# The last expert pair's two tiles in a bank each, and an instruction order drawn with 0.7 instead of 0.8 before TensorE

## The chip, the core and the metric

The kernel runs on one core of a Trainium2 chip. TensorE (PE in the profile) multiplies matrices and writes its results to PSUM, which the kernel divides into eight banks of 128 partitions by 512 floats. VectorE (DVE) and ScalarE (ACT) take results out of the banks. GpSimd (POOL) issues the indirect transfers (gather and scatter), SyncE (SP) the plain ones. The metric is the time of one execution on the device in microseconds (us).

## What is computed

One layer on 2 x 2048 tokens of width 256. The normalised tokens `xn` go through a causal attention made of Chebyshev polynomials and prefix sums, and, in parallel, through a mixture of eight experts, of which each token takes one, plus a shared expert that every token takes:

```python
xn  = _layernorm(x, axis=-1)
x   = x + attn(xn, W_in, W_out) + ffn(xn, ...)
# in ffn, with xf = layernorm(xn) * ln_w + ln_b:
top_idx   = argmax(xf @ router_w, axis=-1);  top_score = sigmoid(max(xf @ router_w))
for e in range(8):
    w    = where(top_idx == e, top_score, 0)[:, None];  xe = xf * w
    acc += (silu(xe @ gate_w[e]) * (xe @ up_w[e])) @ down_w[e]
shared = silu(xf @ sh_gate) * (xf @ sh_up) @ sh_down
```

All of it is in 32-bit floats.

## The kernel before

The tokens are worked in eight chunks `c` of 512 (`NC`), each of four tiles of 128. For every chunk there is a front (normalise, transpose, router), an attention part (`attend`: projections at L1019, head sums at L1049, L1062 and L1067, denominators at L1130 and L1143, output at L1157) and a shared expert (`shared`: gate and up at L955, down at L973). A routing step sorts the tokens into slots by expert. The routed work is then done in units: nine pairs (`pair`: two full tiles of one expert side by side; gate and up at L1258, down at L1271), and single tiles (`expert`: transposes at L1297 and L1320, gate and up at L1307, down at L1328), some of whose tiles are cut into strips of 32 or 64 tokens of different experts. The small matmuls, on 32 or 64 columns of the array, are the head sums and such strips.

A unit ends with a copy of its result from PSUM to a buffer `yt` (L1274 for a pair, L1331 for a single tile) and a scatter to `y_dram` at the tokens' places (`scatter`, L1212, on POOL). The scatters carry a common key, "scatter", so that each waits until the one before it has landed. When all of them have landed, SP loads `y_dram` back in eight pieces (L1354), DVE adds each piece to its chunk `X` (L1363) and SP stores the chunk (L1367). The last chunk is stored in three pieces, and its last two tiles have separate down products and separate adds (L979 to L982), which end the program.

No engine's order is written out by hand. Every step is an `op` with an engine, a cost, the keys it reads and writes, the buffers it takes, and a priority. `Plan.order` plays the steps through in the program's own time: whenever an engine is free, it takes the ready step with the lowest priority number. A step is ready when its inputs are done, plus 0.2 between engines (`CROSS`), or plus 0.8 (`SLACK`) where the step is TensorE's; a buffer or bank is given out again 0.2 after its last user, and the first free one in its pool is taken. The constants decide the order and the places alone; on the chip each engine runs its list in order and waits for semaphores. A change of one constant can therefore move any step on any engine, and give any step another bank.

`bank_p` holds six of the eight PSUM banks; `psq` and `psk` are the other two. In the last pair as in all others, both tiles' down products go to the two halves of one bank `py`, one copy takes the whole bank (ACT, or DVE if it is free first), and two scatters follow.

Of the kernel before, what the change touches and what calls it, by code (L numbers as in the profile page):

```python
# [20 lines left out]
P = 128  # L21
NB, S, D = 2, 2048, 256
# [16 lines left out]
NPAIR = (4 * NTT - 7 * NE) // 8  # L39
# [63 lines left out]
class Plan:  # L103
# [2 lines left out]


    CROSS = 0.2
    SLACK = 0.8
    LAND = 2.2  # L110
    RATE = 280e3
    TABLE = 1.3
# [4 lines left out]
    def op(self, eng, cost, emit, r=(), w=(), a=(), prio=0.0, alloc=(), nbytes=None, alt=(), table=None,  # L117
           after=(), grow=None):

        o = Op()
        o.seq, o.prio, o.alloc, o.nbytes, o.table, o.grow = len(self.ops), prio, list(alloc), nbytes, table, grow
        o.alts = [(eng, cost, emit)] + list(alt)
        need = {}
        for k in r:
            need.update(dict.fromkeys(self.adds.get(k, ())))
            if k in self.last:
                need[self.last[k]] = None
            self.reads.setdefault(k, []).append(o)  # L130
        for k in a:
            if k in self.last:
                need[self.last[k]] = None
            need.update(dict.fromkeys(self.reads.get(k, ())))
            self.adds.setdefault(k, []).append(o)
        for k in w:
            if k in self.last:
                need[self.last[k]] = None
            need.update(dict.fromkeys(self.reads.get(k, ())))
            need.update(dict.fromkeys(self.adds.get(k, ())))  # L140
            self.last[k], self.reads[k], self.adds[k] = o, [], []
        need.pop(o, None)
        o.soon = [n for n in after if n not in need]
        need.update(dict.fromkeys(after))
        o.need, o.after, o.done = need, [], None
        o.bufs = {}
        for k in tuple(r) + tuple(w) + tuple(a):
            b = k[0] if isinstance(k, tuple) else k
            if isinstance(b, Buf):
                o.bufs[b] = None  # L150
        for b in o.alloc:
            b.owner = o
        for b in o.bufs:
            b.users += 1
            if b.owner is not o:
                need[b.owner] = None
        self.ops.append(o)
        return o

    def order(self):  # L160
# [13 lines left out]
        def lat(a, b):  # L174
            return 0.0 if a == b else self.SLACK if b == "PE" else self.CROSS

# [82 lines left out]
def kernel(  # L259
# [107 lines left out]
    bank_p = Pool([ps.tile([P, CH], F32, name=f"bank_{i}") for i in range(6)])  # L367
# [6 lines left out]
    op = plan.op  # L374
    V, A, G, S_, T_ = nc.vector, nc.scalar, nc.gpsimd, nc.sync, nc.tensor
    MM, M256, MT = 0.86, 0.442, 0.115
    KiB = 1024


    FRONT, ROUTE, SCAT, EXQ, SHQ, ATT, EXP, SHA = 0.0, 2.0, 4.0, 6.0, -1.0, 10.0, 30.0, 50.0  # L380
# [10 lines left out]
    for c in range(NC):  # L391
        if c == 0:
            for t in range(NT):
                op("SP", 0.45, lambda t=t: S_.dma_start(out=X[0][:, t, :], in_=x[ts(t, P)]),
                   w=[("X", 0, t)], nbytes=128 * KiB, prio=-90)
# [5 lines left out]
               table="sqrt")  # L401
# [3 lines left out]
               w=["sg"], nbytes=512 * KiB, prio=-88)  # L405
            op("SP", 0.45, lambda: S_.dma_start(out=su, in_=sh_up.rearrange("(k p) f -> p k f", p=P)),
               w=["su"], nbytes=512 * KiB, prio=-87)
        else:
            op("SP", 0.45, lambda c=c: S_.dma_start(
                out=X[c], in_=x[c * CH : (c + 1) * CH].rearrange("(t p) d -> p t d", p=P)),  # L410
               w=[("X", c, t) for t in range(NT)] + [("x_in", c)], nbytes=512 * KiB, prio=-80 + 5 * c)
        if c == 1:
            op("SP", 0.45, lambda: S_.dma_start(out=sd, in_=sh_down.rearrange("(k p) d -> p k d", p=P)),
               w=["sd"], nbytes=512 * KiB, prio=-73)
            op("SP", 0.45, lambda: S_.dma_start(out=w_in, in_=w_in_t.rearrange("(k p) e -> p k e", p=P)),
               w=["w_in"], nbytes=768 * KiB, prio=-74)
        if c == 2:
            op("SP", 0.45, lambda: S_.dma_start(out=w_out, in_=w_out_t.rearrange("(k p) e -> p k e", p=P)),
               w=["w_out"], nbytes=256 * KiB, prio=-68)
# [783 lines left out]
    def gather(e, j, zt):  # L1203
        op("POOL", 1.28, lambda: G.indirect_dma_start(  # L1204
            out=zt.t, out_offset=None, in_=z_dram,
            in_offset=bass.IndirectOffsetOnAxis(ap=take_i[:, j : j + 1], axis=0),
            bounds_check=NTOK - 1, oob_is_err=False,
        ), r=["table"] + [("z_dram", c) for c in range(NC)], w=[zt], alloc=[zt], nbytes=1024 * KiB, prio=EXQ + e - 0.05)

    def scatter(j, yt, src):  # L1210
        def f():
            y_ins.append(G.indirect_dma_start(  # L1212
                out=y_dram, out_offset=bass.IndirectOffsetOnAxis(ap=give_i[:, j : j + 1], axis=0),
                in_=src(), in_offset=None, bounds_check=NTOK - 1, oob_is_err=False,
            ).ins)

        op("POOL", 1.28, f, r=[yt, "table"], w=[("y", j), "scatter"], nbytes=640 * KiB, prio=SCAT)

    def pair(n, j):


        e = 0.1 * n
        ws = [Buf(w_p, f"{m}_{j}") for m in ("wg", "wu", "wd")]
        wg, wu, wd = ws
        zts = [Buf(zt_p, f"zt_{j + i}") for i in range(2)]
        sc = Buf(zt_p, f"sc_{j}")
        xT, yt = Buf(h_p, f"xT_{j}"), Buf(h_p, f"yt_{j}")
        pz, py = Buf(bank_p, f"pz_{j}"), Buf(bank_p, f"py_{j}")
        weights(e, [j // 2], [ws])
        for i in range(2):  # L1230
            gather(e, j + i, zts[i])
        op("POOL", 1.0, lambda: G.dma_start(
            out=sc.t.rearrange("p (i q) -> p i q", i=2),
            in_=score_dram[j : j + 2].unsqueeze(0).to_broadcast([P, 2, P])),
           r=["score_dram"], w=[sc], alloc=[sc], nbytes=128 * KiB, prio=EXQ + e - 0.04)
        for i in range(2):
            def f(i=i):
                for k in range(KD):
                    T_.transpose(pz.t[:, ds(k * 2 * P + i * P, P)], zts[i].t[:, ts(k, P)], ident)  # L1239
            op("PE", 2 * MT, f, r=[zts[i]], w=[(pz, i)], alloc=[] if i else [pz, xT], prio=EXQ + e)  # L1240
        for k in range(KD):
            op("ACT", 0.46, lambda k=k: A.activation(
                xT.t[:, ts(k, 2 * P)], pz.t[:, ts(k, 2 * P)], AF.Identity, bias=lnb[:, k : k + 1],
                scale=lnw[:, k : k + 1]), r=[(pz, 0), (pz, 1), "ln"], w=[(xT, k)], prio=EXQ)

        def f():
            v = xT.t.rearrange("p (k t) -> p k t", k=KD)
            V.tensor_tensor(v, v, sc.t.unsqueeze(1).to_broadcast([P, KD, 2 * P]), ALU.mult)
        X2 = [(xT, 0), (xT, 1)]
        op("DVE", 0.69, f, r=X2 + [sc], w=X2, prio=EXQ)  # L1250
        sls = []
        for h in range(2):
            pg, pu, sl = Buf(bank_p, f"eg_{j + h}"), Buf(bank_p, f"eu_{j + h}"), Buf(h_p, f"sl_{j + h}")

            def mm(b, wt, h=h):
                for f in range(2):
                    for k in range(KD):
                        T_.matmul(b.t[:, ts(f, 2 * P)], wt.t[:, ds(k * FF + (2 * h + f) * P, P)], xT.t[:, ts(k, 2 * P)],  # L1258
                                  start=(k == 0), stop=(k == KD - 1))
            op("PE", 4 * M256, lambda mm=mm, pg=pg: mm(pg, wg), r=X2 + [wg], w=[pg], alloc=[pg, pu], prio=EXP + e)  # L1260
            o = op("PE", 4 * M256, lambda mm=mm, pu=pu: mm(pu, wu), r=X2 + [wu, pg], w=[pu], prio=EXP + e - 0.2)
            op("ACT", 0.62, lambda sl=sl, pg=pg: A.activation(sl.t, pg.t, AF.Silu), r=[pg], w=[sl], alloc=[sl],
               prio=EXQ, table="silu")
            op("DVE", 0.69, lambda sl=sl, pu=pu: V.tensor_tensor(sl.t, sl.t, pu.t, ALU.mult), r=[pu, sl], w=[sl],
               prio=EXQ)
            sls.append(sl)
        ups.append(o)
        for i in range(2):
            def f(i=i):
                for f in range(KF):  # L1270
                    T_.matmul(py.t[:, ts(i, D)], sls[f // 2].t[:, ds(f % 2 * 2 * P + i * P, P)], wd.t[:, ts(f, D)],  # L1271
                              start=(f == 0), stop=(f == KF - 1))
            op("PE", 4 * M256, f, r=sls + [wd], w=[(py, i)], alloc=[] if i else [py], prio=EXQ + 10 + e)
        op("ACT", 0.6, lambda: A.copy(yt.t, py.t), r=[(py, 0), (py, 1)], w=[yt], alloc=[yt], prio=EXQ,  # L1274
           alt=[("DVE", 0.69, lambda: V.tensor_copy(yt.t, py.t))])
        for i in range(2):
            scatter(j + i, yt, lambda i=i: yt.t[:, ts(i, D)])

    def expert(n, j):
        e = 0.1 * n  # L1280
# [44 lines left out]
        def f():  # L1325
# [6 lines left out]
           alt=[("DVE", 0.42, lambda: V.tensor_copy(yt.t, py.t[:, :D]))])  # L1332

        scatter(j, yt, lambda: yt.t)


# [13 lines left out]
    for c in range(NC):  # L1350
        b = Buf(w_p, f"y_{c}")

        def f(c=c, b=b):
# [11 lines left out]
           r=[b], a=keys, prio=60 + c)  # L1365
        for t, n in ((0, 2), (2, 1), (3, 1)) if c == NC - 1 else ((0, NT),):
            op("SP", 0.45, lambda c=c, t=t, n=n: S_.dma_start(  # L1367
                out=out[ds(c * CH + t * P, n * P)].rearrange("(t p) d -> p t d", p=P), in_=X[c][:, t : t + n, :]),
               r=keys[t : t + n], w=[("out", c, t)], nbytes=n * 104 * KiB, prio=60 + c)
# [40 lines left out]
```

## Time and profile before

| | us |
|---|---|
| median of 3 runs | 564.18 (564.17 to 564.25) |
| the profiled execution | 564.25 |
| its span, first to last instruction | 562.5 |
| PE busy | 554.8 |
| DVE busy | 489.0 |
| ACT busy | 222.1 |
| POOL busy | 101.0 |

The span leaves out 1.75 us of the execution that lie before its first and after its last instruction. The granted TensorE clock is 0.998 of full speed over the span. TensorE's busy time counts from the start of a weight load or matmul to its modelled end, so that pieces which stand close together merge into one; a matmul of 32-bit floats shows as two instructions, and a group marked x8 is four matmuls.

### The profile page before, as it was taken

To read this page: it belongs to the slowest core of one execution; us is meant where nothing else is said; L and a number is where in the kernel's file an instruction comes from. 1 tells how busy PE (TensorE), PEld (TensorE's weight loads), DVE (VectorE), ACT (ScalarE), POOL (GpSimd) and SP (SyncE) were. 2 spreads that over 40 slices of the span, in tenths; PEclk is the share of its full clock that TensorE was granted. 3 is DMA by queue.
4 is the path that set the end of the run, shared out by engine and by line. 5 is a ranking of instruction groups with operands and counts; after the bars stand their busy time and mean duration, and the time that the engine had idled before them with its cause. 6 is when DMAs were issued, how large, how long until landed. Compare 5 with 4: busy or idle time off the path is not lost.

```text
span 562.5 us, 8132 instructions
## 1 busy us (share of the span) xinstructions
PE 554.8 (99%) x2760; PEld 324.5 (58%) x2760; DVE 489.0 (87%) x814; ACT 222.1 (39%) x430; POOL 101.0 (18%) x123
## 2 busy tenths in 40 slices
PE   7999999999999999999999999999999999999996
PEld 7564465665457575556547545756645474368754
DVE  6899898998999999999999989899999989677236
ACT  4869761012552344235333524442363353212000
POOL 4210100005142330231114122113101100112100
PEclk9999999999999999999999999999999999999999
DMA  8857651147658993884499287829836871950098
GB/s 277 284 169 261 226 225 37 45 147 266 184 193 286 313 367 89 275 276 170 145 352 327 87 272 262 304 57 316 293 102 209 275 261 24 297 194 19 27 296 302
DMA packets 78505, 119.71 MB, mean 213 GB/s; under 512 B 5416, under 2 KB 47199, under 8 KB 78464
## 3 DMA queue, kind: packets, MB, share of 16 engines
q1 hardware_dynamic: 73504, 107.49, 56.7%
q0 software_dynamic: 4416, 11.70, 6.9%
q8 instruction: 22, 0.36, 0.3%
q14 instruction: 19, 0.16, 0.1%
q10 hardware_dynamic: 544, 0.00, 0.1%
HBM read 100.28 MB, written 19.16 MB: 212 GB/s over the span
## 4 chain that ended last, share of the span: by engine, by line
PE 98%; DVE 1%; DMA 0%; ACT 0%; issue 0%
PE bank L955 20%; PE bank L1019 15%; PE bank L1258 11%; PE bank L1307 11%; PE bank L973 10%; PE bank L1271 6%; PE bank L1328 6%; PE bank L1157 5%; PE psk L1049 3%; PE psq L1049 2%; PE bank L1320 1%; PE bank L557 1%; PE psk L1062 1%; PE bank L1239 1%; PE bank L897 1%; PE psk L1143 1%
## 5 line engine op out<-in xcount | busy, mean ns | idle before, releaser
L1019 PE MATMUL bank<-xnT,w_in 128*128 128x512 f32 x192 | 87.3, 595 | 0.0
L1086 DVE TENSOR_TENSOR_SCAN tv<-ones,carry,tv 128x512 f32<-128x512 f32 x60 | 76.7, 1278 | 1.0
L1307 PE MATMUL bank<-big,wide 128*32 128x512 f32 (+2 forms) x288 | 64.0, 598 | 0.0
L1212 POOL DMA_INDIRECT y_dram<-wide,give_i x28 | 33.7, 1205 | 166.2 <-ACT wide L1274 63.2
L955 PE MATMUL bank<-xfT,sg 128*128 128x512 f32 (+1 forms) x136 | 60.8, 572 | 1.1 <-ACT xfT L535 1.1
L955 PE MATMUL bank<-xfT,su 128*128 128x512 f32 (+1 forms) x136 | 61.0, 573 | 0.0
L1258 PE MATMUL bank<-wide,big 128*128 128x256 f32 x256 | 58.5, 381 | 0.0
L1019 PEld LDWEIGHTS bank<-xnT,w_in 128*128 128x128 f32 x192 | 35.5, 190 | 39.8 <-issue 36.2
L973 PE MATMUL bank<-sd,hT 128*128 128x256 f32 x256 | 57.8, 381 | 0.0
L1258 PEld LDWEIGHTS bank<-wide,big 128*128 128x128 f32 x256 | 47.9, 190 | 10.5 <-issue 3.9
L973 PEld LDWEIGHTS bank<-sd,hT 128*128 128x128 f32 x256 | 47.8, 190 | 8.8 <-issue 1.6
L962 ACT ACTIVATE hT<-bank 128x512 f32<-128x512 f32 x32 | 19.0, 596 | 75.5 <-PE bank L955 75.4
L1106 DVE TENSOR_TENSOR o<-o,tv 128x512 f32<-128x512 f32 x64 | 44.2, 691 | 1.5
L1204 POOL DMA_INDIRECT wide<-z_dram,take_i x20 | 25.2, 1258 | 89.0 <-DVE give_i L922 72.9
L955 PEld LDWEIGHTS bank<-xfT,sg 128*128 128x128 f32 x136 | 24.6, 190 | 26.6 <-issue 23.5
L955 PEld LDWEIGHTS bank<-xfT,su 128*128 128x128 f32 x136 | 24.8, 190 | 24.2 <-issue 22.4
L1041 DVE SCALAR_TENSOR_TENSOR T<-T 128x1024 f32<-128x1024 f32 x32 | 37.8, 1216 | 0.0
L1027 ACT ACTIVATE T<-bank 128x512 f32<-128x512 f32 x32 | 19.1, 596 | 45.3 <-PE bank L1019 45.1
L1307 PEld LDWEIGHTS bank<-big,wide 128*32 128x32 f32 (+2 forms) x288 | 19.1, 128 | 29.0 <-issue 27.6
L964 DVE TENSOR_TENSOR hT<-hT,bank 128x512 f32<-128x512 f32 x32 | 21.8, 683 | 12.4 <-PE bank L955 12.4
L1083 DVE TENSOR_TENSOR tv<-T 128x512 f32<-128x512 f32 x48 | 32.4, 674 | 0.1
L990 DVE TENSOR_TENSOR X<-X,bank 128x512 f32<-128x512 f32 x31 | 21.1, 680 | 11.9 <-PE bank L973 7.8
(266 smaller groups left out, 923.1 us busy)
## 6 DMA issues: line engine op xcount, KB each, us to landing
big<-in_up_w SPq DMA_DIRECT2D x47, 512.0 KB, 5.4
big<-in_gate_w SPq DMA_DIRECT2D x41, 512.0 KB, 5.7
big<-in_down_w SPq DMA_DIRECT2D x40, 512.0 KB, 6.4
z_dram<-big SPq DMA_DIRECT2D x8, 512.0 KB, 4.5
xfT<-in_down_w SPq DMA_DIRECT2D x8, 512.0 KB, 5.4
X<-in_x SPq DMA_DIRECT2D x7, 512.0 KB, 9.3
xn_dram<-xnT SPq DMA_DIRECT2D x7, 512.0 KB, 3.3
xnT<-xn_dram SPq DMA_DIRECT2D x7, 512.0 KB, 8.6
```

The source lines that it names most:

```text
L955: T_.matmul(b.t[:, cols], wt[:, k, ts(f, P)], vx(k)[:, cols], start=(k == 0), stop=(k == KD - 1))
L973: T_.matmul(po.t[:, ts(i, D)], hT[f].t[:, ts(tp * 2 + i, P)], sd[:, f, :], start=(f == 0), stop=(f == KF - 1))
L1019: T_.matmul(pm.t, w_in[:, k, ds(i * D + g * P, P)], xnT.t[:, ts(k, CH)], start=(k == 0), stop=(k == KD - 1))
L1041: op("DVE", 1.27, lambda i=i, j=j, q=part: V.scalar_tensor_tensor(q[i](), q[j](), off[i], q[1](), ALU.subtract, ALU.mult), r=[(T, j)] + X2 ...
L1083: V.tensor_tensor(b.t, q[i](1), v(), ALU.mult)
L1086: o_ = op("DVE", 1.25, lambda b=b, i=i, g=g: V.tensor_tensor_scan(b.t, ones[:, 0:1].to_broadcast([P, CH]), b.t, 0.0 if opening else old[:, ...
L1106: op("DVE", 0.66, lambda o=o, b=b: V.tensor_tensor(o(), o(), b.t, ALU.add), r=[b, ok], w=[ok], prio=p)
L1212: y_ins.append(G.indirect_dma_start(out=y_dram, out_offset=bass.IndirectOffsetOnAxis(ap=give_i[:, j : j + 1], axis=0), in_=src(), in_offse ...
L1258: T_.matmul(b.t[:, ts(f, 2 * P)], wt.t[:, ds(k * FF + (2 * h + f) * P, P)], xT.t[:, ts(k, 2 * P)], start=(k == 0), stop=(k == KD - 1))
L1271: T_.matmul(py.t[:, ts(i, D)], sls[f // 2].t[:, ds(f % 2 * 2 * P + i * P, P)], wd.t[:, ts(f, D)], start=(f == 0), stop=(f == KF - 1))
L1307: T_.matmul(b.t[n, :], xT.t[:, ds(k * P + n.start, n.stop - n.start)], wt.t[:, ts(k, FF)], start=(k == 0), stop=(k == KD - 1), skip_group_ ...
L1328: T_.matmul(py.t[n, :D], hmT.t[:, ds(i * P + n.start, n.stop - n.start)], wd.t[:, ts(i, D)], start=(i == 0), stop=(i == KF - 1), skip_grou ...
```

## The change

`SLACK` is 0.7 instead of 0.8, so every step of every engine is ordered anew. In the last pair (`j == 2 * NPAIR - 2`), the two tiles take a bank each (`pys`), ACT copies each tile's 128x256 result by itself after that tile's four down matmuls, and each scatter waits for its own copy; DVE is no longer an alternative for these copies. The other pairs are written as before.

```diff
-    SLACK = 0.8
+    SLACK = 0.7
...
-    def scatter(j, yt, src):
+    def scatter(j, yt, src, key=None):
...
-        op("POOL", 1.28, f, r=[yt, "table"], w=[("y", j), "scatter"], nbytes=640 * KiB, prio=SCAT)
+        op("POOL", 1.28, f, r=[key or yt, "table"], w=[("y", j), "scatter"], nbytes=640 * KiB, prio=SCAT)
...
+        last = j == 2 * NPAIR - 2
+        pys = [py, Buf(bank_p, f"py_{j + 1}")] if last else [py, py]
         for i in range(2):
             def f(i=i):
                 for f in range(KF):
-                    T_.matmul(py.t[:, ts(i, D)], sls[f // 2].t[:, ds(f % 2 * 2 * P + i * P, P)], wd.t[:, ts(f, D)],
+                    T_.matmul(pys[i].t[:, ts(i, D)], sls[f // 2].t[:, ds(f % 2 * 2 * P + i * P, P)], wd.t[:, ts(f, D)],
                               start=(f == 0), stop=(f == KF - 1))
-            op("PE", 4 * M256, f, r=sls + [wd], w=[(py, i)], alloc=[] if i else [py], prio=EXQ + 10 + e)
-        op("ACT", 0.6, lambda: A.copy(yt.t, py.t), r=[(py, 0), (py, 1)], w=[yt], alloc=[yt], prio=EXQ,
-           alt=[("DVE", 0.69, lambda: V.tensor_copy(yt.t, py.t))])
+            op("PE", 4 * M256, f, r=sls + [wd], w=[(pys[i], i)], alloc=[] if i and not last else [pys[i]],
+               prio=EXQ + 10 + e)
+            if last:
+                op("ACT", 0.4, lambda i=i: A.copy(yt.t[:, ts(i, D)], pys[i].t[:, ts(i, D)]), r=[(pys[i], i)],
+                   w=[(yt, i)], alloc=[] if i else [yt], prio=EXQ)
+        if not last:
+            op("ACT", 0.6, lambda: A.copy(yt.t, py.t), r=[(py, 0), (py, 1)], w=[(yt, 0), (yt, 1)], alloc=[yt], prio=EXQ,
+               alt=[("DVE", 0.69, lambda: V.tensor_copy(yt.t, py.t))])
         for i in range(2):
-            scatter(j + i, yt, lambda i=i: yt.t[:, ts(i, D)])
+            scatter(j + i, yt, lambda i=i: yt.t[:, ts(i, D)], (yt, i))
```

The lines behind the pair move down by up to eight: L1271 becomes L1274, the whole-bank copy L1282, the single copies L1279, L1297 becomes L1305, L1307 L1315, L1320 L1328, L1322 L1330, L1328 L1336, L1354 L1362, L1363 L1371 and L1367 L1375. The text below uses the numbers of before, except where it says otherwise.

## The prediction
> **What bounds the kernel now.** I read the page's busy times first, then the chain that ended last, then the chain in order of time, then the timeline and the windows of the last 35 us.
>
> ```profile
> PE 554.8 (99%) x2760; PEld 324.5 (58%) x2760; DVE 489.0 (87%) x814; ACT 222.1 (39%) x430; POOL 101.0 (18%) x123
> ...
> PE 98%; DVE 1%; DMA 0%; ACT 0%; issue 0%
> ```
>
> TensorE is the bound, and hardly ever waits: 98% of the chain is its own work. So there is almost no wait to win, and whatever lengthens TensorE's list lengthens the kernel. The chain in order of time shows what on that list isn't multiplication:
>
> ```profile
> 213.76 1.00 PE psk L1049 x8
> 214.76 0.86 PE psq L1049 x8
> 215.62 3.65 PE bank L1258 x16
> ...
> 429.71 0.59 ACT wide L1322
> 430.35 1.99 PE bank L1328 x8
> ...
> 511.17 3.45 PE bank L1258 x16
> ```
>
> Columns: start, length, piece. L1258 x16 takes 3.45 us among full matmuls (the last line), but 3.65 with a group of 32-column matmuls before and after it; L1049 x8 takes 1.00 as the first such group, 0.86 as the second. One visit to the small matmuls thus costs 0.20 + 0.14 = 0.34 us beyond its work, however long it is. ACT in the chain is the one real wait after the first 9 us: L1328 waits for the copy L1322. By the starts, the L1130 group ahead of it occupies 0.84 us where its six other visits alone take 0.45, so the wait is 0.39.
>
> The end, by the timeline:
>
> ```profile
> 528.91 0.69 DVE L1275 COPY tv<-bank 128x512 f32<-128x512 f32 x1 [4.41 <-PE bank L1271]
> 529.87 0.98 POOL L1212 DMA_INDIRECT y_dram<-tv,give_i  x1 [9.63 <-DVE tv L1275]
> 532.56 0.98 POOL L1212 DMA_INDIRECT y_dram<-tv,give_i  x1 [1.70 <-DMA y_dram<-tv,give_i]
> 535.05 1.47 SPq L1354 DMA_DIRECT2D big<-y_dram  x3
> 546.31 12.72 SPq L1367 DMA_DIRECT2D out<-X  x10
> 551.06 7.07 PE L973 MATMUL bank<-sd,hT 128*128 128x256 f32 x32
> 558.17 0.42 DVE L981 TENSOR_TENSOR X<-X,bank 128x256 f32<-128x256 f32 x1 [0.49 <-PE bank L973]
> ```
>
> and by the windows of the last microseconds (engine busy times, granted clock, DMA share, GB/s):
>
> ```profile
> 558.00:559.00 1.00, 0.13 (x1) 0.00 (x0) 0.42 (x1) 0.00 (x0) 0.00 (x0) 1.00 1.05 345
> 559.00:560.00 1.00, 0.00 (x0) 0.00 (x0) 0.00 (x0) 0.00 (x0) 0.00 (x0) 1.00 1.03 345
> 560.00:561.00 1.00, 0.00 (x0) 0.00 (x0) 0.00 (x0) 0.00 (x0) 0.00 (x0) 0.64 0.30 102
> ```
>
> TensorE ends at 558.13, DVE's last add at 558.59, and the last store is issued behind it at 558.62. It lands at 561.37, 2.75 us later; 1.17 us of closing semaphores follow. The DMA engines are full until after 560: that store stands behind the stores of earlier chunks. So the time is 558.13 of TensorE's list, 4.4 behind it, and 1.75 outside the span.
>
> **The change part by part**, against the profiled execution's 564.25 us.
>
> *The last pair's copies and scatters.* TensorE's 16 instructions at L1271 stay; they go to two banks. DVE's copy of 0.69 (L1275) goes, two ACT copies of 0.37 come (L1331, the same 128x256 shape, x15, mean 0.372). ACT idles here (8.0 us before L962 at 525.45), so neither price is on the path. The first tile's product ends 8 x 0.216 = 1.73 before the second's. Copies start 0.2 after a product's last matmul, POOL follows a copy by 0.27 (529.60 to 529.87), a scatter lands in 2.42 and the next is issued 0.27 later. From the second product's end: first scatter at -1.73 + 0.20 + 0.37 + 0.27 = -0.89, second at -0.89 + 2.42 + 0.27 = 1.80, landed 4.23, loads at 4.29. Before, it was 528.87 to 535.05, that is 6.18. So 1.9 us are saved there. In the new program's order on TensorE, the last pair's down products also stand two gate/up steps (2 x 1.72) earlier, ahead of 4 instead of 2 such steps before the L973 groups. Counted from TensorE's end, the loads go out 1.9 + 3.4 = 5.3 us earlier. POOL has nothing behind these scatters, and SP only the loads and stores.
>
> *What that is worth.* The loads were already hidden under TensorE, so the 5.3 us themselves are worth nothing. What they do is let the chunk stores run out before the last store. In the new DVE order the first add of a loaded piece stands behind both L990 of chunk 6, done 18 us before TensorE's end; the loads' first landing (3.9 us after issue before) comes 24 us before it, so DVE doesn't wait, and the gate/up banks that DVE frees behind that add are not late. Chunk 6's store then goes out some 6.5 us before TensorE's end, not 2.7. The last store is alone, or nearly. Its price alone isn't in the trace. Upper bound: the 2.75 of before (no gain). Lower: 512 KB stores to `xf_dram` landed in 2.62 when the queues were quiet; less 384 KB at the 345 GB/s of the window above (1.1 us) leaves 1.5, an estimate, and a gain of 1.2. `X<-in_x` loads of the same 128 KB landed in 2.56 to 2.66 at the start, a direction that is further off. I take 2.05, a gain of **0.7**. The Trainium skill (DMA: Bandwidth & Descriptors, Anatomy of one DMA) says that a transfer has a fixed cost of about 2.0 us, most of it the receipt of the last write. By that rule the store would take some 2.4 (estimate: 2.0 plus 128 KB at the measured rate) and the gain be 0.35.
>
> *The new order: visits to the small matmuls.* I compared the two programs' orders on TensorE. Leaving out lone transposes of a few rows, the list goes from full matmuls to the small kinds 58 times before and 62 times after: 4 x 0.34 = +1.36. Two details. The 0.34 holds where a full matmul follows; where transposes follow (19 visits before, 9 after), the starts show 0.055 in place of 0.104 behind the visit: 10 x 0.05 = +0.49. And two of the four come from parting a joint visit of L1143 with another kind, which costs 0.095, not 0.23, in front: 2 x -0.14 = -0.28. Sum **+1.57**, all on the path; bounds 1.0 (the four at 0.25 alone) and 1.9. The Trainium skill (TensorEngine Tiling (Array Packing), Key Properties) says that changing the tiling mode, not merely the tile, drains TensorE. That speaks against this change, and agrees in kind with the 0.34; it has no figure, so the sum by it is the row's.
>
> *The new order: banks.* Where a step takes the bank that TensorE itself filled just before, it waits for the copy: 0.2 from the last matmul to ACT's start, 0.59 the copy, 0.05 to TensorE, 0.84 in all (L1320, L1322, L1328 above). Before, every such reuse has at least 0.87 us of other TensorE work between, except the 0.39 wait. In the new order, once, in chunk 3, four transposes (L1320) into bank 5 are followed at once by L1019 into bank 5: 0.84, nothing between. Once, in chunk 4, L1019 reuses bank 2 with six transposes (0.655) between: about 0.85 - 0.655 = 0.2. The old wait at L1328 has no counterpart. Net 0.84 + 0.2 - 0.39 = **+0.65**; bounds -0.4 (both covered by something I don't see) and 1.3.
>
> *The new order: 0.1 less before TensorE.* In before's trace L1271 started at 525.25, 0.76 after its input (L1264, 523.81 + 0.69), without a gap, and at 430.30 the release took 0.05. A tenth less seldom bites; I take **+0.1**, with bounds 0 and 1.6 (four waits of 0.39). Weight loads and gathers: no wait for them in before; none added.
>
> *Sum*: 564.25 + 1.57 + 0.65 + 0.1 - 0.7 = 565.87; the execution profiled is 0.07 above the median, so **565.8**.
>
> **Rivals.** (a) *No difference.* The last store gains the full 1.2, the bank waits are covered: 564.18 + 1.57 - 0.39 + 0.1 - 1.2 = 564.3. For it: the DMA share of 1.05 at 558. Against: bank 5 stands bare in the order. (b) *Faster.* The end is set by the drained stores, and a visit costs nothing extra when its neighbours are ready: without the 1.57 and the bank waits 564.18 - 0.39 - 1.2 = 562.6. It decides from visits below 0.1 each. Against it: 0.34 repeats at every L1049 visit in the chain. (c) *The shorter slack bites often*: six more waits of 0.39 on a list without reserve give 565.8 + 2.3 = 568.1. For it: nothing else fills an in-order list. Against: one wait in 550 us so far. (d) *The split does nothing*, since the scatters remain in series; its own gain of 1.9 wasn't on the path, and without the 0.7 it is 566.5.
>
> **How the numbers follow.** 0.2% of this kernel, about what a measurement can tell from no change, is 1.13 us. Forecast with (d), 564.9 to 567.0: 0.60, of which some 0.08 lie under 565.3; (c) 0.16; (a) 0.18; (b) 0.06. Slower by over 0.2%: 0.52 + 0.16 = 0.68; within: 0.18 + 0.08 = 0.26; faster: 0.06. The range leaves out (b), the lower part of (a) and the far end of (c): 564.3 to 567.7.
>
> **What would show it.** Right: the L1019 that opens chunk 3 waits some 0.8 us for the copy L1330 (new line) and shows as ACT in the chain; TensorE ends 2.2 us later, near 560.4; the chain shows 3.65 and 1.00 more often; the y loads go out some 28 us before TensorE's end; the last store lands in about 2 us. Wrong: if TensorE ends by 559, the visits or the bank waits are mispriced; above 562, waits that I didn't see; if the last store still needs 2.7, its price was the path's own and not the queue's.

## The result, and the profile after

The changed kernel takes 565.11 us (median of 20 executions, 565.01 to 565.49); before took 564.23 beside it (20 executions, 564.00 to 564.73). The ratio is 1.0015, with a 95% interval of 1.0009 to 1.0021: slower by 0.9 us, on the side that was forecast, by less than the 1.13 us called what a measurement can tell, and 0.7 us under the predicted 565.8. The time is inside the range and inside the forecast case's own 564.9 to 567.0.

The profiled execution took 565.17 us, its span 563.4. The page, with the busy times, the share of the chain, and the one group of L1019 that now has a releaser:

```profile
PE 557.1 (99%) x2760; PEld 324.6 (58%) x2760; DVE 489.3 (87%) x810; ACT 226.5 (40%) x435; POOL 99.2 (18%) x123
...
PE 98%; DVE 1%; DMA 0%; ACT 0%; issue 0%
...
L1019 PE MATMUL bank<-xnT,w_in 128*128 128x512 f32 x192 | 88.8, 598 | 0.7 <-ACT wide L1330 0.7
```

TensorE has the same 2760 instructions and is busy 2.3 us longer. The idle column of L1019 names the new wait: the copy L1330. The chain in order of time shows it at its place, the opening of chunk 3 (start, length, piece):

```profile
235.98 0.45 PE bank L1328 x4
236.43 0.02 issue
236.45 0.59 ACT wide L1330
237.05 0.04 issue
237.09 5.42 PE bank L1019 x12
```

The transposes L1328 fill a bank, ScalarE empties it, L1019 takes the same bank. Against an unbroken list the first L1019 starts 0.84 us late, and its first matmul takes 0.104 us longer than the others. Now the end, by the timeline:

```profile
525.60 0.37 ACT L1279 COPY tv<-bank 128x256 f32<-128x256 f32 x1 [1.13 <-PE bank L1274]
526.24 0.98 POOL L1212 DMA_INDIRECT y_dram<-tv,give_i  x1 [7.58 <-ACT tv L1279]
529.40 0.98 POOL L1212 DMA_INDIRECT y_dram<-tv,give_i  x1 [2.18 <-DMA y_dram<-tv,give_i]
531.87 0.92 SPq L1362 DMA_DIRECT2D big<-y_dram  x2
542.95 17.87 SPq L1375 DMA_DIRECT2D out<-X  x10
560.02 0.42 DVE L981 TENSOR_TENSOR X<-X,bank 128x256 f32<-128x256 f32 x1 [1.30 <-PE bank L973]
```

and by the windows (stretch, its length, busy time of PE, PEld, DVE, ACT and POOL with instructions, clock, DMA share, GB/s):

```profile
557.00:558.00 1.00, 1.00 (x6) 0.88 (x5) 0.25 (x1) 0.00 (x0) 0.00 (x0) 1.00 0.00 0
...
560.00:561.00 1.00, 0.00 (x0) 0.00 (x0) 0.42 (x1) 0.00 (x0) 0.00 (x0) 1.00 0.02 5
561.00:562.00 1.00, 0.00 (x0) 0.00 (x0) 0.00 (x0) 0.00 (x0) 0.00 (x0) 1.00 0.39 131
```

TensorE ends at 559.98 instead of 558.13. The loads of `y_dram` are issued 28.1 us before that (before: 23.1). From 557 to 558 the DMA engines stand still; at 561 they move only the last store, which is issued 0.49 behind TensorE's end as before, lands about 1.73 later instead of 2.75 (an estimate: no landing of it is on record, so it is reckoned back from the end of the span with the 1.17 that follow the landing in before; the store just ahead of it, of the same size, took 1.71), and closes the program 3.40 after TensorE's end, not 4.42. So the kernel loses 1.85 us on TensorE and wins 1.02 behind it.

An accounting of TensorE's starts says where the 1.85 us are: each step's start to the next one's, less what the same matmuls take among their own kind (0.429 us for 128x512, 0.216 for 128x256, and so on). A bubble is the time by which the first matmul behind a visit, or behind a wait, takes longer than its kind. The accounting counts five narrow groups more than the prediction did, before and after alike.

| TensorE from 9.2 us on, us | before | after | difference |
|---|---|---|---|
| full matmuls and transposes, steady | 431.95 | 431.95 | 0 |
| work of the small matmuls | 88.55 | 88.55 | 0 |
| visits to them: 63 and 67, in front and inside | 22.25 | 22.82 | +0.57 |
| bubbles of 0.104 behind a visit: 40 and 46 | 4.16 | 4.79 | +0.63 |
| bubbles of 0.055 behind a visit: 19 and 17 | 1.07 | 0.95 | -0.12 |
| bubbles without a visit (0.08 at 291; 0.104 behind each new wait) | 0.08 | 0.21 | +0.13 |
| waits (0.39 at 430; 0.84 at 237 and 0.20 at 292) | 0.39 | 1.03 | +0.64 |

Nothing else changed: +1.08 from the visits and +0.77 from the waits with their bubbles.

### The profile page after: what moved, and what is told of

The parts are those of the page before. It is cut to its first block, busy times and chain, and to the rows that moved or that the text cites. A ratio compares the mean times of both kernels' runs of the same rounds, so it can differ in the third digit from the quotient of the medians.

```text
span 563.4 us, 8141 instructions
## 1 busy us (share of the span) xinstructions
PE 557.1 (99%) x2760; PEld 324.6 (58%) x2760; DVE 489.3 (87%) x810; ACT 226.5 (40%) x435; POOL 99.2 (18%) x123
## 4 chain that ended last, share of the span: by engine, by line
PE 98%; DVE 1%; DMA 0%; ACT 0%; issue 0%
PE bank L955 20%; PE bank L1019 15%; PE bank L1258 11%; PE bank L1315 11%; PE bank L973 10%; PE bank L1274 6%; PE bank L1336 6%; PE bank L1157 5%; PE psk L1049 3%; PE psq L1049 3%; PE bank L1328 1%; PE psk L1062 1%; PE bank L557 1%; PE bank L1305 1%; PE psk L1143 1%; PE bank L897 1%
## 5 line engine op out<-in xcount | busy, mean ns | idle before, releaser
L1019 PE MATMUL bank<-xnT,w_in 128*128 128x512 f32 x192 | 88.8, 598 | 0.7 <-ACT wide L1330 0.7
L1212 POOL DMA_INDIRECT y_dram<-wide,give_i x32 | 38.5, 1204 | 191.9 <-ACT wide L1282 98.6
L1315 PE MATMUL bank<-big,wide 128*32 128x512 f32 (+2 forms) x280 | 62.4, 597 | 0.0
L1019 PEld LDWEIGHTS bank<-xnT,w_in 128*128 128x128 f32 x192 | 35.0, 190 | 38.7 <-issue 32.3
L1258 PE MATMUL bank<-wide,big 128*128 128x256 f32 x208 | 48.2, 384 | 0.0
L1258 PEld LDWEIGHTS bank<-wide,big 128*128 128x128 f32 x208 | 38.6, 190 | 9.7 <-issue 3.3
L1204 POOL DMA_INDIRECT wide<-z_dram,take_i x20 | 23.8, 1188 | 99.2 <-DVE wide L921 75.1
L964 DVE TENSOR_TENSOR hT<-hT,bank 128x512 f32<-128x512 f32 x32 | 21.8, 685 | 17.3 <-PE bank L955 16.8
L1315 PEld LDWEIGHTS bank<-big,wide 128*32 128x32 f32 (+2 forms) x280 | 18.6, 127 | 27.1 <-issue 25.8
L1092 ACT COPY carry<-tv 128x1 f32<-128x1 f32 x80 | 15.2, 190 | 46.7 <-DVE tv L1086 46.5
```

The source lines that it names most:

```text
L1019: T_.matmul(pm.t, w_in[:, k, ds(i * D + g * P, P)], xnT.t[:, ts(k, CH)], start=(k == 0), stop=(k == KD - 1))
L1212: y_ins.append(G.indirect_dma_start(out=y_dram, out_offset=bass.IndirectOffsetOnAxis(ap=give_i[:, j : j + 1], axis=0), in_=src(), in_offse ...
L1315: T_.matmul(b.t[n, :], xT.t[:, ds(k * P + n.start, n.stop - n.start)], wt.t[:, ts(k, FF)], start=(k == 0), stop=(k == KD - 1), skip_group_ ...
```

## The experiments

Times are medians beside before on the same chips (564.24 to 564.28). Line numbers are those of the changed kernel. In e3 to e9 the lists are taken as the planner drew them, and single steps are put directly behind another one on the same engine; all other orders stay. The diff is shortened: the list of pairs stands in the call itself, and from e5 on `pe` is the list of the moved step's own engine.

```diff
-    for _, _, emit in plan.order():
+    for _, _, emit in regroup(plan.order(), moves):
         emit()
...
+        for what, behind in moves:
+            pe.remove(what)
+            pe.insert(pe.index(behind) + 1, what)
```

The numbers in `moves`, shown below for each kernel, are steps in the order in which the program defines them.

**e1: the split without the new slack.**

```diff
-    SLACK = 0.7
+    SLACK = 0.8
```

> The split copies and scatters alone, SLACK left at 0.8. On TensorE the list is that of before but for the last pair: 58 visits to the small matmuls as before, the wait at the transposes' copy near 430 us (0.39) as before. Theory (the split is worth only what it does to the last store, and the redraw is what costs): TensorE ends at 558.1 as before, the y loads go out 1.9 us earlier (some 25.0 before TensorE's end, not 23.1), the last store lands in about 1.75 instead of 2.75, time 563.2 (-1.0). Rival (the 1.0 comes from the redraw, which moves the last pair's down products two steps forward; the split alone doesn't clear the store queue): last store still 2.5 or more, time 564.0 to 564.3.

Measured: 563.21 (563.16 to 563.81), ratio 0.9983 (0.9974 to 0.9992). TensorE's accounting is before's to 0.02 us in every row, its end 558.08, and 3.40 us follow it.

```profile
527.13 0.37 ACT L1279 COPY tv<-bank 128x256 f32<-128x256 f32 x1 [1.13 <-PE bank L1274]
527.78 0.98 POOL L1212 DMA_INDIRECT y_dram<-tv,give_i  x1 [7.59 <-ACT tv L1279]
530.95 0.98 POOL L1212 DMA_INDIRECT y_dram<-tv,give_i  x1 [2.19 <-DMA y_dram<-tv,give_i]
533.43 1.48 SPq L1362 DMA_DIRECT2D big<-y_dram  x3
```

```profile
558.00:559.00 1.00, 0.08 (x1) 0.00 (x0) 0.42 (x1) 0.00 (x0) 0.00 (x0) 1.00 0.34 115
```

In this timeline the loads go out 24.65 us before TensorE's end, 1.6 earlier than before. That is enough to empty the store queue: in the window in which TensorE ends, the DMA share is 0.34, where before had 1.05. Alone, the split is worth 1.0 us; the slack's redraw is the whole loss.

**e2: the new slack without the split.** Before, with one line changed:

```diff
-    SLACK = 0.8
+    SLACK = 0.7
```

> SLACK 0.7 alone, the last pair written as before (one bank, one copy, then both scatters). 62 visits and both bank waits (0.84 near 236 us, 0.2 near 292 us) as in the changed kernel. Theory A (the split is what clears the store queue): TensorE ends at 560.0, the last store lands in 2.75 again, time 566.1. Theory B (either the split or the two steps that the redraw moves the pair forward is enough to clear the queue): TensorE ends at 560.0, last store 1.75 to 2.0, time 565.1 to 565.4, so the split is worth nothing on top of the redraw. If the redraw weren't what costs, 564.2 or less.

Measured: 565.05 (564.99 to 565.11), ratio 1.0015 (1.0006 to 1.0024), the changed kernel's time. TensorE ends at 559.98 again, and again 3.40 us follow. The timeline of this kernel (its lines are numbered as before's):

```profile
527.32 0.69 DVE L1275 COPY tv<-bank 128x512 f32<-128x512 f32 x1 [4.41 <-PE bank L1271]
528.29 0.98 POOL L1212 DMA_INDIRECT y_dram<-tv,give_i  x1 [9.63 <-DVE tv L1275]
533.44 0.92 SPq L1354 DMA_DIRECT2D big<-y_dram  x2
```

With the whole copy the loads still go out 26.5 us before the end, since the redraw put the last pair's products two steps earlier. The queue needs clearing only once: either part does it, and the second finds nothing left. In the change as made, the split brings nothing.

**e3: more visits.** The changed kernel with ten steps of TensorE moved, so that a full matmul step stands between two small ones:

```diff
+    moves = [(1119, 1681), (1124, 1138), (573, 1203), (612, 1207), (667, 1272),
+             (761, 1341), (800, 1354), (949, 1471), (988, 1489), (1506, 1711)]
```

> The changed kernel with nothing altered but the order of TensorE's own list at ten places: a full matmul group is moved from behind a visit to the small matmuls into its middle. 70 visits instead of 62; no work added. Theory (a visit costs 0.34 us beyond its work, whatever its length): +2.6 us, 567.7, with 1.86 in front of and inside the visits and 0.78 behind them. Rival (what lengthened TensorE's list was waits, and a visit is free if its neighbours are ready): within 0.5 us of 565.1. A reservation: steps that start up to 1.7 us later can make others wait; waits show in the trace and are subtracted.

Measured: 568.66 (568.61 to 568.70), ratio 1.0078 (1.0063 to 1.0094); TensorE ends at 563.50, 3.5 later. The accounting has eight visits more: 2.80 in front and inside, 0.78 in bubbles. A part of the 2.80 is a wait that the parting opened, as the chain in order of time shows:

```profile
197.26 1.98 PE bank L1315 x16
...
199.34 0.76 DVE xfT L1323
...
200.15 0.66 PE bank L1328 x4
```

Between the end of L1315 at 199.24 and L1328's start at 200.15 TensorE has nothing to do but wait for VectorE; by the starts that step is some 1.1 us longer than such a step and its bubble are elsewhere. The eight visits thus cost 3.58 - 1.1 = 2.5, or 0.31 each.

**e4: fewer visits.** The changed kernel with seventeen joins, 49 visits by the prediction's count of 62:

```diff
+    moves = [(291, 290), (328, 189), (330, 329), (270, 267), (385, 384), (422, 385), (1059, 424), (1249, 1248),
+             (1313, 736), (1314, 1313), (1378, 800), (855, 854), (893, 892), (894, 893), (1444, 1443), (1505, 988),
+             (1018, 1506)]
```

> The changed kernel with TensorE's list reordered at 17 places so that neighbouring visits become one: 49 visits instead of 62, the same work. Each moved step had its inputs and bank ready before its new place in the changed kernel's trace. Theory (0.34 a visit): -4.2 us, 560.9, less what the steps behind a longer visit wait for. Rival (visits free): 565.1 or slower. If the time falls by less than 2 and the trace shows new waits, the visits' price stands and the order costs elsewhere.

Measured: 567.62 (567.26 to 567.93), ratio 1.0058 (1.0043 to 1.0073): a miss by over 6 us. The page of waits of this kernel (engine, tile, line, releaser; total, times, longest) and the one long piece of its chain:

```profile
PE bank L1019 <- ACT T L1027: 0.9, 2, 0.5
...
PE bank L973 <- DVE xnT L564: 0.7, 1, 0.7
PE bank L1315 <- DMA big<-in_up_w: 0.7, 1, 0.7
```

```profile
327.78 5.06 DMA big<-in_up_w
```

Five new waits outside the visits sum to 3.1 us (0.89 at 67.1, 0.52 at 186.0, 0.63 at 290.1 and 344.0, 0.45 at 346.5): steps that had stood between a result and its use were taken away from there. A sixth lies inside a joined visit at 327.9, where 32 small matmuls take 6.8 us instead of 2 x 1.85, since the weights of the second half, whose buffer the visit's first half frees, land at 332.8. The bubbles behind the five and a small wait at 350.5 add 0.6. These 6.8 us more than undo what 13 visits less brought (6.8 less the 2.8 by which the list grew: 4.0, or 0.31 each). The price of a visit stands; a join is only free where nothing needs the cover that it removes.

**e5: the store queue filled again.** The changed kernel with VectorE's adds of `y` back in before's places behind the products L964:

```diff
+    moves = [(1751, 1735), (1754, 1751), (1757, 1739), (1760, 1757), (1763, 1743), (1766, 1763), (1769, 1766)]
```

> The changed kernel with one thing put back: VectorE's order at the end is before's (the adds of the chunks of y stand behind the same products with hT as before), so the nine chunk stores start late again, with a full store queue at the last one; the split, the schedule and TensorE's order stay as changed. Theory A (the tail fell by 1.0 us because the store queue is empty when the last store is issued): TensorE's end stays at 559.98, the last store takes about 2.75 us again instead of 1.73, the median is 565.11 + 1.0 = 566.1. Rival B (the tail is shorter for another reason, the split copies or the earlier loads of y by themselves): the last store keeps its 1.73 us and the median stays at 565.1.

Measured: 566.00 (565.72 to 566.12), ratio 1.0031 (1.0019 to 1.0042). TensorE ends at 559.93; 4.31 us follow instead of 3.40. The windows of this kernel:

```profile
560.00:561.00 1.00, 0.00 (x0) 0.00 (x0) 0.39 (x1) 0.00 (x0) 0.00 (x0) 1.00 1.05 354
561.00:562.00 1.00, 0.00 (x0) 0.00 (x0) 0.00 (x0) 0.00 (x0) 0.00 (x0) 1.00 1.03 344
```

The split, the early scatters and the early loads are all there; only VectorE's adds and with them the chunk stores are late, the queue is full when the last one is issued at 560.42, 0.49 behind TensorE's end as in the changed kernel, and 0.9 us are back. So the tail's gain is the queue's, and not that of the split or of the early loads by themselves.

**e6: the bare bank wait covered.** The changed kernel with the sixteen instructions of one L1143 group (head weights of chunk 2) put between the transposes and the L1019 that waits:

```diff
+    moves = [(550, 1162)]
```

> The changed kernel with one step of TensorE moved: the sixteen small matmuls of L1143 at 227.7 (0.73 us, the head weights of chunk 2) now stand between the transposes of L1328 at 235.98 and the first matmul of L1019 at 237.09. The number of visits stays 62. Theory A (the 0.84 us ahead of L1019 is only the way from the transposes over ScalarE's 0.59 us copy back to the bank, and any step put there covers it): the wait falls by about 0.75 to under 0.1, TensorE ends at 559.2, median 565.11 - 0.75 = 564.35. Rival B (ScalarE's queue, not missing cover, sets the time, so the wait moves along with what is put in, or the later head weights make VectorE and the next steps wait): the median stays at 565.1 or rises.

Measured: 564.25 (564.11 to 564.84), ratio 1.0001 (0.9992 to 1.0010). The chain at the place:

```profile
235.13 0.44 PE bank L1328 x4
235.57 0.30 PE psk L1143
...
236.22 0.02 issue
236.24 5.42 PE bank L1019 x12
```

No ACT piece is left; L1019 starts 0.67 us behind the end of L1328, with work in between. The accounting lost the 0.84 wait whole, TensorE ends at 559.14, and the kernel is 0.86 us faster than the changed one. One step in another place pays back the whole change's loss, beside a before of 564.27.

**e7: joins that open no wait.** The split with slack 0.8 (e1) and four joins:

```diff
+    moves = [(261, 258), (1054, 1053), (548, 1183), (761, 760)]
```

> The split with the old slack of 0.8 (563.21 us measured alone), with four steps of TensorE put directly behind a neighbouring visit to small matmuls: 54 visits instead of 58. Chosen so that nothing behind the place where a step is taken out needs its cover. Theory A (a visit costs its 0.3 to 0.34 us wherever it stands, and the joined version that came out slower lost its gain to bank and weight waits that the joins had opened): 563.21 - 4 x 0.31 = 562.0, TensorE's end 558.08 - 1.24 = 556.8, no new wait over 0.15. Rival B (visits are not what costs; taking them away brings nothing that lasts): 563.2 or more.

Measured: 562.40 (562.33 to 562.86), ratio 0.9970 (0.9958 to 0.9981), 0.81 under e1 where 1.24 was expected. The accounting fell by 0.87. Three joins gave what a visit costs (0.23 each in front and inside, and behind 0.104 once and 0.055 twice; 0.91 in all, or 0.30 each); the fourth, of two L897 groups, lost 0.05: by the timeline the second group waits for VectorE,

```profile
112.81 1.14 PE L897 MATMUL bank<-big 128*64 128x136 f32 x14
114.12 1.14 PE L897 MATMUL bank<-big 128*64 128x136 f32 x14 [0.17 <-DVE big L891]
```

where a visit of one such group has 0.35 us beyond its work in front and inside, and the joined one has 0.86, 0.15 more than two apart, against a bubble of 0.10 less.

**e8: a reordered list.** e1 with thirty steps moved, ordered by the durations of e1's trace, for 45 visits:

```diff
+    moves = [(167, 291), (290, 167), (360, 1623), (261, 258), (362, 1665), (1068, 1674), (1134, 414), (1198, 454),
+             (456, 1097), (1180, 1119), (1124, 1099), (1183, 548), (1184, 562), (1245, 1328), (1329, 1164), (550, 1189),
+             (1285, 1224), (736, 1694), (1319, 752), (760, 1342), (761, 760), (1521, 800), (1440, 1379), (830, 1702),
+             (832, 846), (1384, 832), (1419, 882), (1502, 1444), (1471, 978), (1505, 986)]
```

> The split with the old slack of 0.8, with 30 steps of TensorE between 58 and 490 us moved so that there are 45 visits to small matmuls instead of 58; every other engine keeps its order. Theory A: 13 visits x 0.31 = 4.0 us less, against which up to 1.3 us stand at 184 us (transposes of L984 waiting for VectorE's L1323) and up to 0.6 at 388 us: TensorE's end 558.08 - 2.9 = 555.2, median 563.21 - 2.9 = 560.3, between 559.2 with no new wait and 561. Rival B (as in the first joined version, waits for banks and weights take more than the visits give): 563.2 or more.

Measured: 565.66 (564.12 to 567.75), ratio 1.0020 (1.0007 to 1.0032), a miss by 5 us. The timeline of TensorE, and the windows around it:

```profile
247.29 0.69 PE L1239 MATMUL bank<-ident,xfT 128*128 128x128 f32 x2 [3.35 <-DMA xfT<-z_dram,take_i]
...
248.63 2.87 PE L955 MATMUL bank<-xfT,sg 128*128 128x512 f32 x4
```

```profile
244.00:247.20 3.20, 0.00 (x0) 0.00 (x0) 3.16 (x5) 0.36 (x1) 1.02 (x1) 1.00 1.17 342
247.20:249.00 1.80, 1.71 (x7) 1.67 (x8) 1.29 (x1) 0.09 (x1) 0.74 (x1) 0.50 0.80 289
249.00:250.00 1.00, 1.00 (x2) 0.34 (x1) 0.00 (x0) 0.50 (x1) 0.36 (x1) 0.50 1.08 424
```

One moved transposition freed a gather's buffer only at 240.3, and the gather, for which I had reckoned with 2.5 us, took 6.69 among full DMA queues. That was no exception: before's gathers (L1204) land in 2.8 to 7.9 us, 5.3 at the median. TensorE stood 3.35 us, and then ran at a granted clock of 0.50 for some 3.4 us. By the starts, 4.3 us are waits outside the visits, 3.5 of them this one, and the half clock makes the matmuls behind it some 1.6 us longer. The rest of the list behaved as in e4 and e7: visits and the bubbles behind them fell by 2.9 for 13 visits, although an inner wait takes 0.25 of it back.

**e9: five joins.** e1 again, without the L897 join and with two other joins:

```diff
+    moves = [(1054, 1053), (548, 1183), (761, 760), (1471, 931), (1505, 948)]
```

> The split with the old slack of 0.8 and five steps of TensorE joined to a neighbouring visit: three of the four joins of the version before (the join of L897, which had opened a wait of 0.50 us for VectorE's L891, is left out) and two more, at 470 us (a pair's L1272 behind L1154) and at 477 us (L1318 behind L1047): 53 visits instead of 58. Theory A (0.336 us a visit, as the three joins without a new wait gave): 563.21 - 5 x 0.336 = 561.5, TensorE's end 558.08 - 1.68 = 556.4, the accounting of visits and bubbles 27.95 - 1.68 = 26.27. Rival B (the joins that paid were chance; further ones pay nothing): 562.2 or more.

Measured: 562.14 (562.04 to 562.31), ratio 0.9962 (0.9948 to 0.9975): the fastest version here, 2.1 us under before and 3.0 under the changed kernel. TensorE ends at 556.71, 1.37 before e1's; the accounting fell by 1.40 for five visits less, 0.28 each where 0.336 was expected. That price was mine from e7 and too high: it credited the fourth join's bubble to the other three, which gave 0.30 each. The median fell by 1.07 only, since the part of the execution outside the span is 2.04 us here and 1.71 in e1; no run shows why. The last two rows of this kernel's waits of TensorE (engine, tile, line, releaser; total, times, longest):

```profile
PE psq L530 <- DVE big L510: 0.3, 1, 0.3
PE bank L1336 <- ACT wide L1330: 0.3, 1, 0.3
```

No wait is new: e1 has the same two. The 1.40 are 1.02 in front and inside (0.20 a visit) and 0.38 behind (two bubbles of 0.104 and three of 0.055), where the 0.336 had reckoned with 0.23 and 0.104 at each. The median alone does not rule out rival B, 562.2 or more, since the runs reach 562.31; by the accounting the two added joins gave 0.49 on top of the three's 0.91, so further joins did pay.

## Why the prediction came out as it did

*Right: the mechanism and the side.* TensorE's list sets the time, the redraw lengthens it by visits and by one bare bank, and the drained stores give back a part. e2 shows that the redraw alone makes the loss, e1 that the split alone would be a gain.

*The visits: right in kind, mis-sized.* Predicted +1.57, measured +1.08. The count of four more visits holds, and the price of 0.34 nearly does: e3's eight parted ones came to 0.31 each, e4's thirteen to 0.31, e7's three joined ones to 0.30, e9's five to 0.28. Rival (b), below 0.1 each, is out. What failed is the second detail, "where transposes follow (19 visits before, 9 after)": the trace after has 17 bubbles of 0.055, not 9. The transposes L1305 of single tiles follow a visit too, and I had not counted them in the new order. With 17 that detail is +0.10 in place of +0.49, and the term 1.36 + 0.10 - 0.28 = 1.18; most of the last 0.1 lies in front and inside, 0.57 where the prediction's prices make 0.64, and why is open.

*The bank waits: right, but for their bubbles.* Predicted 0.84 + 0.2 - 0.39 = 0.65; measured 0.839 at 237.1, 0.195 at 292.3 and the old 0.39 gone, 0.64. The 0.104 behind each of the two, where before has one of 0.08, were not in the prediction: 0.77 with them. e6 shows that the first is lack of cover and no more: 0.65 us of other work took it away.

*The shorter slack: +0.1 predicted, 0 measured.* No other wait of TensorE appeared in the accounting. So rival (c), six further waits, did not happen.

*The last store: right in kind, mis-sized.* Predicted -0.7, measured -1.02: the store alone lands in 1.73, not 2.05; the lower bound of 1.5 was nearer than the value taken from `X<-in_x` loads and `xf_dram` stores. The rule of the Trainium skill (DMA: Bandwidth & Descriptors, Anatomy of one DMA), about 2.0 us of fixed cost, would have given 2.4. That section and its fit are about transfers that GpSimd issues, while this store is issued by SyncE, which the prediction did not say; the 1.71 measured, and the estimate of 1.73, with all 128 KB in them show that the figure does not carry over to it. e5 shows that the gain is the empty queue.

*The split's share.* The prediction gave the 5.3 us earlier loads as 1.9 by the split plus 3.4 by the redraw, and priced their effect once. Measured are 5.0: 1.6 by the split (e1) and 3.4 by the redraw (e2). The split brought less since the second scatter went out 3.16 us behind the first, where the prediction's steps make 2.69. But rival (d), "the split does nothing", is in a sense true: not because the scatters stay in series, but because the redraw clears the queue alone (e2). As a forecast of time (d), 566.5, was wrong: the store's gain came all the same.

*The sum.* 564.25 + 1.08 + 0.77 + 0 - 1.02 = 565.08 against 565.17 in the profiled execution; the other 0.09 lie outside the span. The prediction's sum of 565.87 is 0.8 more: 0.5 in the visits, 0.1 in the slack and 0.3 in the store, less 0.1 for the bubbles behind the waits. That is also why the case given most weight, slower by more than 0.2%, was not what came: 0.9 us is 0.15%. Rival (a) was right that the difference stays under 0.2%, but for the wrong reason, and its 564.3 is no nearer than the forecast: it had the bank waits covered and the store gain full; the waits came and the store gain nearly did.

*Left open.* That full DMA queues made the gather of e8 slow was only read from the DMA share of 1.17 beside it, not tried. Whether a list with 45 visits and no such stall would reach 560 was not tried either.

## What to carry to other kernels

When one in-order engine is 98% of the chain, count what a reordering does to its list: changes of kind and bank reuses without work in between, each by its own measured price, and look where each change leads. Two edits that clear the same queue must be credited once; run each alone before believing that both work. A step that seems to be free to move is often the cover for another step's copy, gather or weight load: a join pays only where nothing behind the gap needs it.

## What the runs showed of the hardware that was not expected

- A stop of TensorE of 3.35 us cost more than itself in e8: the granted clock fell to 0.50 for some 3.4 us, and two 128x512 matmuls in a row took 0.85 us each instead of 0.43. The executions of e8 fall in two groups by their mean clock: five at 1.000 took 564.1 to 564.4 us, seven at 0.994 to 0.997 took 565.5 to 567.8. Only one of the seven was profiled, so whether TensorE stood as long in the five is not known. A stop of 1.03 us (e3) left the clock alone. The Trainium skill (TensorE: Matmul & The Clock Gate, Part 1: The HAM clock gate) gives half rate after an idle window of about 3.4 us. The half rate agrees; the stop was no longer than such a window, though, and at the program's end the clock falls 2.2 us behind TensorE's last matmul in before and 2.0 in after, so here less than 3.4 us was enough.
- A 128 KB store to DRAM landed in 1.71 us on a nearly empty queue (after, 558.74; the last store's 1.73 is the estimate above), behind full queues in 2.75 (before's last store).
- Joining two 64-column groups whose operands VectorE makes just in time cost 0.05 us more than it saved: one visit less (0.35 in front and inside, 0.10 behind), a wait of 0.50 more (e7).
